# One-table layer norms, the last values inside the score loop's start, and a transposed inverse turned by VectorE, in a six-layer perceiver kernel

## The chip, the cores and the metric

The kernel runs on one core of one Trainium2 chip. The time is device microseconds of one execution. The kernel before took 768.55 us, the median of three runs (767.87 to 768.75).

## The reference

The input x is 128 x 256, the context 12544 x 256, all float32. Six residual layers follow one another, each on a layer norm of x:

```python
x = x + _L0_xattn_ref(_layernorm(x), ctx, mask, ...)   # 4 heads of 64, over the context
x = x + _L0_attn_ref(_layernorm(x), ...)               # gated delta net, 12 heads, 64 x 128 states
x = x + _L0_ffn_ref(_layernorm(x), ...)                # 8 experts, the best one
x = x + _L1_xattn_ref(_layernorm(x), ctx, ...)         # 16 heads of 16, over the context
x = x + _L1_attn_ref(_layernorm(x), ...)               # linear attention with a decay scan, gated
x = x + _L1_ffn_ref(_layernorm(x), ...)                # 8 experts, the best two

def _layernorm(x, axis=-1, eps=1e-05):
    m = jnp.mean(x, axis=axis, keepdims=True)
    v = jnp.var(x, axis=axis, keepdims=True)
    return (x - m) / jnp.sqrt(v + eps)
```

The delta net's step over 128 rows is a recurrence. The kernel solves it for all rows at once, which needs, for each head, the inverse of a 128 x 128 unit triangular matrix.

## The kernel before

The rows of x lie on the 128 partitions. The context is worked through in 24 blocks of 512 rows and one of 256. The first attention (`xattn0_first`) makes keys (L404), values (L417), scores (L438) and weighted sums (L465) block by block and keeps the context in SBUF. The second attention needs keys and values of the same context. They depend only on weights, so a `Filler` hands them out in small units as work for TensorE wherever it would wait: `fill(n)` issues the next n units. A block has eight of them: four for two key tiles `pk` (L1027, two units a tile), which ScalarE copies to `kh` (L1034) and a DMA stores in DRAM, and four for two value tiles `pv` (L1048), which ScalarE copies into the place of the context (L1053, shown as `ctx<-pv`). Both kinds rotate through two PSUM banks, so a third tile waits until ScalarE has copied the first.

From the first attention's end to the second attention's start the order on TensorE and ScalarE is the order of the code (`manual_schedule`); other engines are ordered by a scheduler. Whatever stands between two operations in the code stands between them in the queues.

**Layer norm** (`layernorm`, L134). VectorE computes mean and variance; ScalarE computes the inverse root as exp(-0.5 ln(v + eps)) (`rsqrt`); VectorE makes the normed `h`; TensorE transposes it (L151). Ln and Exp come from two function tables here, "natural_log" and "exp_and_others", each brought in by an ACT_TABLE_LOAD. Fill units are issued between these steps. The last two layers have a norm of their own (`root`, L1339 to L1351) with a Newton step behind the two activations and one table, "natural_log_exp_and_others", which holds both functions and is loaded once at the end of the second attention (L1137).

**The inverse** (L815 to L845). The 32 x 32 blocks on the diagonal are inverted by doubling, in four levels after a first one. `t` holds the inverse, `tt` its transpose, both in the tile `inv`. Each level multiplies in three sets of 48 small products, 96 passes on TensorE each:

```python
each(px, lambda r, h, c: am[r, h, :], t, four_tiles)
xs = block("xs")
nc.scalar.mul(xs, px, -1.0)
```

Then `py` from `tt` and `xs` is added to `t`, and `pyt` from `xs` and `tt` is added to `tt`, with two fill units behind each set. Afterwards blocks of 64 rows are put together in the same way (L874 to L891), from copies `t64` and `ttf` that POOL makes of `t` and `tt`. After level 0 `t` is made from `tt` by one VectorE transposition in blocks of 32 (L830).

**From the filler to the scores of the second attention.** `xattn1_first` computes queries and their maxima, issues all remaining units (`fill(None)`), gives the filler's two banks back (`close`), and calls `weigh1`. There each chunk of 128 context rows has 64 score products (L1101) into four banks, `st1` (one bank, one buffer) and `st3` (three banks, two buffers), two exponentials on ScalarE (L1107) into `e`, and the weighted sums (L1118) into the bank `ot`, which a product of zeros (L1091) clears first. Scores run two chunks ahead of the sums: scores(0), scores(1), then for each chunk i scores(i + 2) and the sums of i.

**The tail** (`last_layers`). After the last sums ScalarE copies `ot` (L1141). The result is turned and divided. `beat(n)` (L1359) issues n products of 256 columns, two passes each, whose result is never read. Seven of them stand ahead of the fifth layer's norm.

Of the kernel before, what the change touches and what calls it, by code (L numbers as in the profile page):

```python
# [11 lines left out]
F32 = mybir.dt.float32  # L12
# [3 lines left out]
AF = mybir.ActivationFunctionType  # L16
ALU = mybir.AluOpType
# [55 lines left out]
def network(ctx: ExitStack, tc: tile.TileContext, a: dict, y_out, bad):  # L73
# [45 lines left out]
        )  # L119


    def rsqrt(dst, src, bias, scale=1.0, fill=None):


        if fill:
            nc.scalar.preload_act_table_set("natural_log")
            fill(2)
        nc.scalar.activation(dst, src, AF.Ln, bias=bias, scale=scale)
        if fill:
            nc.scalar.preload_act_table_set("exp_and_others")  # L130
            fill(2)
        nc.scalar.activation(dst, dst, AF.Exp, scale=-0.5)

    def layernorm(x, psum, tag, fill=None):  # L134

        stats = small.tile([S, 6], F32, tag="ln_stats", name="ln_stats")
        nc.vector.bn_stats(stats, x)
        mv = small.tile([S, 2], F32, tag="ln_mv", name="ln_mv")
        nc.vector.bn_aggr(mv, stats)
        rstd = small.tile([S, 1], F32, tag="ln_rstd", name="ln_rstd")  # L140
        if fill:
            fill(1)
        rsqrt(rstd, mv[:, 1:2], eps[:S, 0:1], fill=fill)
        h = act.tile([S, D], F32, tag="h", name="h", bufs=1)
        nc.vector.tensor_scalar(h, x, mv[:, 0:1], rstd, ALU.subtract, ALU.mult)
        hT = act.tile([128, KC, S], F32, tag="hT", name="hT", bufs=1)
        if fill:
            fill(4)
        pt = psum.tile([128, 512], F32, tag=tag, name="ln_pt")
        for k in range(KC):  # L150
            nc.tensor.transpose(pt[:, k * S : (k + 1) * S], h[:, k * 128 : (k + 1) * 128], ident)  # L151
        nc.vector.tensor_copy(hT.rearrange("p k s -> p (k s)"), pt[:, : KC * S])
        if fill:
            fill(1)
        return hT
# [418 lines left out]
    def delta_net(x, wqkv, fill):  # L574
# [7 lines left out]
        with (  # L582
# [136 lines left out]
            nc.scalar.preload_act_table_set("exp_and_others")  # L719
# [105 lines left out]
            for li in range(len(LEVELS)):  # L825
                am = block("am")
                nc.gpsimd.tensor_mul(am, atc, m_blk[:, li, :].unsqueeze(1).to_broadcast([128, NH, 32]))
                if li == 0:
                    nc.vector.tensor_sub(tt, m_blk[:, len(LEVELS), :].unsqueeze(1).to_broadcast([128, NH, 32]), am)
                    nc.vector.transpose(  # L830
                        flat[:, :384], flat[:, 384:768]
                    )
# [12 lines left out]
                nc.vector.tensor_add(tt, tt, pyt)  # L845
                fill(2)


# [87 lines left out]
    def experts(x, wr, bias_row, we, be_src, top, y=None, fill=lambda n: None):  # L936

        with (
# [6 lines left out]

            be = mp.tile([NE, D], F32, name="be")
            nc.sync.dma_start(be, be_src)
            hT = layernorm(x, psp, "ps", fill)
# [115 lines left out]
    def weigh1(x, qs, kss, cp, sp, loaded, late):  # L1064

        H, DH, G = 16, 16, 4
        with (
            tc.tile_pool(name="x1_e", bufs=1) as ep,  # L1070
            tc.tile_pool(name="x1_st", bufs=1, space=PSUM) as ps_st,
        ):
            xb = cp.tile([S, D], F32, name="xb")
# [17 lines left out]
            nc.tensor.matmul(ot.rearrange("p g s -> p (g s)"), zl, zr, start=True, stop=False)  # L1091

            def scores(i):
                b, c = chunks[i]
                e = ws[i % 3]
                st1 = ps_st.tile([128, 1, G, S], F32, tag="st1", name="st1")
                st3 = ps_st.tile([128, 3, G, S], F32, tag="st3", name="st3", bufs=2)
                for g in range(G):
                    for j in (1, 2, 3, 0):
                        r = slice(32 * j, 32 * j + 32)  # L1100
                        nc.tensor.matmul(  # L1101
                            st3[:, j - 1, g, :] if j else st1[:, 0, g, :],
                            kss[b % 3][r, g // 2, g % 2, c * 128 : (c + 1) * 128], qs[r, g, :],
                            start=True, stop=True,
                        )
                for st, j in ((st1, slice(0, 1)), (st3, slice(1, 4))):
                    nc.scalar.activation(  # L1107
                        e[:, j].rearrange("p j g s -> p (j g s)"),
                        st.rearrange("p j g s -> p (j g s)"), AF.Exp,
                    )  # L1110
                return e
# [13 lines left out]
            for b in range(loaded, 2):  # L1125
                load1(kss, b)
            with tc.manual_schedule(engines={PE, ACT}):
                es = [scores(0), scores(1)]
                for i, (b, c) in enumerate(chunks):
                    if c == 0 and b + 2 < NB:  # L1130
                        load1(kss, b + 2)
                    if c == 0 and b == 12:
                        late()
                    if i + 2 < len(chunks):
                        es.append(scores(i + 2))
                    attend(i, es.pop(0))
                nc.scalar.preload_act_table_set("natural_log_exp_and_others")  # L1137

            oT = cp.tile([128, G, S], F32, name="oTs")
            for g in (0, 2):  # L1140
                nc.scalar.copy(oT[:, g : g + 2], ot[:, g : g + 2])  # L1141
            pt = ps_st.tile([128, 1, G, S], F32, tag="st1", name="pt")[:, 0].rearrange("p g s -> p (g s)")
# [55 lines left out]
    def xattn1_first(x, wq, filler, close, late):  # L1198

        fill = filler.fill  # L1200
        H, G = 16, 4
        with (
            tc.tile_pool(name="x1_c", bufs=1) as cp,
            tc.tile_pool(name="x1_s", bufs=2) as sp,
            tc.manual_schedule(engines={PE, ACT}),
        ):
            qs = cp.tile([128, G, S], F32, name="qs")
            kss = strips1(cp)
            load1(kss, 0)
# [98 lines left out]
    def last_layers(x, w, total):  # L1308
# [4 lines left out]
        with (  # L1313
# [114 lines left out]
            for m in range(KC):  # L1428
# [9 lines left out]
            nc.scalar.preload_act_table_set("natural_log_exp_and_others")  # L1438
            beat(2)
            away = both()  # L1440
            nc.vector.tensor_sub(away, o, v)
# [127 lines left out]
    class Filler:  # L1569
# [2 lines left out]

        def __init__(self, kp):
            self.kp, self.units = kp, self.steps()

        def steps(self):
            for b in range(NB if bad is not None else EARLY):
# [11 lines left out]
        def fill(self, n):  # L1589

            for _ in self.units if n is None else islice(self.units, n):
                pass

    with tc.tile_pool(name="k1", bufs=3) as kp:
        filler = Filler(kp)
# [136 lines left out]
```

## Time and profile before

| what | value |
|---|---|
| median of three runs | 768.55 us |
| profiled execution | 771.03 us |
| its span | 769.0 us |
| mean granted TensorE clock | 0.994 |
| DMA traffic, mean over the span | 74 GB/s |

| stage, us from the span's start | length | TensorE busy |
|---|---|---|
| first attention's loop, 30 to 265 | 235.00 | 234.49 |
| its end and the delta net's norm, 265 to 299 | 34.00 | 32.61 |
| delta net up to the inverse, 299 to 348 | 49.00 | 48.38 |
| inverse, 348 to 393 | 45.00 | 42.59 |
| rest of the delta net and the experts, 393 to 457 | 64.00 | 64.00 |
| second attention's norm and queries, 457 to 470 | 13.00 | 12.05 |
| remaining units, 470 to 523.3 | 53.30 | 53.30 |
| passage to the scores, 523.3 to 533.1 | 9.80 | 8.28 |
| score loop, 533.1 to 730 | 196.90 | 196.90 |
| end of the loop and the last two layers, 730 to 769 | 39.00 | 29.18 |

A matrix product of float32 runs as several passes, and the profile counts passes: one of 256 columns takes about 0.215 us, one of 512 about 0.43. In the profile's rows the bracket at the end gives how long the engine was idle before the row and what ended that time; "issue" means that nothing the profile shows was waited for. PE is TensorE's products, PEld its weight loads, DVE VectorE, ACT ScalarE, POOL GpSimd, SP the engine that issues most DMAs.

### The profile page before, as it was taken

To read this page: it belongs to the slowest core of one execution; us is meant where nothing else is said; L and a number is where in the kernel's file an instruction comes from. 1 tells how busy PE (TensorE), PEld (TensorE's weight loads), DVE (VectorE), ACT (ScalarE), POOL (GpSimd) and SP (SyncE) were. 2 spreads that over 40 slices of the span, in tenths; PEclk is the share of its full clock that TensorE was granted. 3 is DMA by queue.
4 is the path that set the end of the run, shared out by engine and by line. 5 is a ranking of instruction groups with operands and counts; after the bars stand their busy time and mean duration, and the time that the engine had idled before them with its cause. 6 is when DMAs were issued, how large, how long until landed. Compare 5 with 4: busy or idle time off the path is not lost.

```text
span 769.0 us, 23891 instructions
## 1 busy us (share of the span) xinstructions
PE 748.8 (97%) x10861; PEld 562.1 (73%) x10861; DVE 221.1 (29%) x405; ACT 406.9 (53%) x491; POOL 234.7 (31%) x192
## 2 busy tenths in 40 slices
PE   8999999999999999999999999999999999999985
PEld 4677777777777867666667757667888888888873
DVE  2444444433444444972114142000000000000045
ACT  2433433333444424654224432336999999999941
POOL 5686666667776632314012021000000000000000
PEclk9999999999999999999999999999999999999998
DMA  9970000000000012333010345211432222222000
GB/s 314 384 272 8 6 9 8 8 8 8 9 5 3 1 42 86 110 111 112 31 58 34 103 154 122 94 69 54 132 109 67 70 58 69 72 62 71 6 2 12
DMA packets 36126, 56.70 MB, mean 74 GB/s; under 512 B 5904, under 2 KB 12608, under 8 KB 36016
## 3 DMA queue, kind: packets, MB, share of 16 engines
q1 hardware_dynamic: 35648, 54.05, 22.0%
q8 instruction: 87, 1.43, 0.8%
q0 software_dynamic: 368, 1.03, 0.4%
q14 instruction: 23, 0.19, 0.1%
HBM read 42.09 MB, written 12.98 MB: 72 GB/s over the span
## 4 chain that ended last, share of the span: by engine, by line
PE 91%; DMA 3%; POOL 2%; ACT 2%; issue 1%; DVE 1%; SPq 0%; ACTq 0%; POOLq 0%; DVEq 0%
PE st L1101 14%; PE ot L1118 12%; PE pv L1048 11%; PE pk L1027 11%; PE pv L417 10%; PE pk L404 9%; PE st L438 6%; PE ot L465 6%; PE pr L634 1%; POOL e L451 1%; DMA msk<-in_maskT 1%; PE py L956 1%; PE spare L1359 1%; DMA row<-in_row 1%; DMA m<-in_mask 1%
## 5 line engine op out<-in xcount | busy, mean ns | idle before, releaser
L1107 ACT ACTIVATE e<-st 128x512 f32<-128x512 f32 x196 | 189.7, 1021 | 17.4 <-PE st L1101 16.1
L451 POOL TENSOR_TENSOR e<-e,mk 128x1024 f32<-128x1024 f32 x49 | 115.5, 2357 | 76.1 <-ACT e L445 62.8
L1101 PE MATMUL st<-qs,ks 32*128 32x128 f32 x3136 | 115.8, 283 | 0.8 <-ACT e L1107 0.8
L1101 PEld LDWEIGHTS st<-qs,ks 32*128 32x128 f32 x3136 | 96.9, 186 | 21.4 <-ACT e L1107 20.7
L1118 PE MATMUL ot<-e,ctx 128*17 128x128 f32 x3136 | 105.0, 274 | 0.0
L1048 PE MATMUL pv<-wv,ctx 128*128 128x256 f32 x392 | 92.8, 382 | 2.2 <-ACT kh L1034 1.6
L1027 PE MATMUL pk<-ctx,wk 128*128 128x512 f32 (+1 forms) x200 | 93.4, 591 | 0.8 <-ACT ctx L1053 0.8
L1048 PEld LDWEIGHTS pv<-wv,ctx 128*128 128x128 f32 x392 | 72.9, 190 | 23.5 <-issue 10.7
L456 DVE TENSOR_TENSOR sums<-sums,e 128x1024 f32<-128x1024 f32 x49 | 60.0, 1225 | 100.9 <-POOL e L451 100.9
L417 PE MATMUL pv<-wkv,ctx 128*128 128x256 f32 x392 | 88.3, 383 | 0.0
L1118 PEld LDWEIGHTS ot<-e,ctx 128*17 128x17 f32 x3136 | 77.6, 97 | 12.1 <-ACT e L1107 0.3
L404 PE MATMUL pk<-ctx,wkv 128*128 128x512 f32 (+1 forms) x200 | 86.4, 584 | 0.0
L445 ACT ACTIVATE e<-e 128x1024 f32<-128x1024 f32 x49 | 51.8, 1057 | 65.2 <-DVE e L444 62.4
L417 PEld LDWEIGHTS pv<-wkv,ctx 128*128 128x128 f32 x392 | 73.3, 190 | 11.7 <-PE sc L499 0.8
L447 POOL TENSOR_SCALAR mk<-msk 128x256 f32<-128x256 uint8 x49 | 68.3, 1395 | 4.1
L444 DVE TENSOR_TENSOR e<-st,nm 128x1024 f32<-128x1024 f32 x49 | 56.7, 1218 | 40.7 <-PE st L438 40.7
L1034 ACT ACTIVATE kh<-pk,col 128x512 f32<-128x512 f32 (+1 forms) x50 | 33.8, 679 | 64.7 <-PE pk L1027 63.7
L404 PEld LDWEIGHTS pk<-ctx,wkv 128*128 128x128 f32 x200 | 38.0, 190 | 40.7 <-issue 39.7
L1147 DVE RECIPROCAL den<-pt 128x16 f32<-128x16 f32 x1 | 0.3, 258 | 209.0 <-PE pt L1144 209.0
L1053 ACT COPY ctx<-pv 128x512 f32<-128x512 f32 x49 | 28.7, 586 | 53.8 <-PE pv L1048 53.7
L1027 PEld LDWEIGHTS pk<-ctx,wk 128*128 128x128 f32 x200 | 36.0, 190 | 28.4 <-issue 24.0
L408 ACT COPY kT<-pk 128x1024 f32<-128x1024 f32 (+1 forms) x25 | 24.9, 996 | 58.7 <-PE pk L404 58.7
(324 smaller groups left out, 622.9 us busy)
## 6 DMA issues: line engine op xcount, KB each, us to landing
ctx<-in_ctxT SPq DMA_DIRECT2D x24, 512.0 KB, 8.3
kd<-kh SPq DMA_DIRECT2D x48, 256.0 KB, 2.0
ks<-kd SPq DMA_DIRECT2D x192, 64.0 KB, 2.7
w<-in_L_ffn_expert_w SPq DMA_DIRECT2D x4, 512.0 KB, 3.8
ctx<-in_L_ffn_We SPq DMA_DIRECT2D x4, 512.0 KB, 4.0
msk<-in_maskT SPq DMA_DIRECT2D x24, 64.0 KB, 1.8
w<-in_L_attn_Wqk SPq DMA_DIRECT2D x2, 768.0 KB, 10.1
w<-in_L_attn_Wv SPq DMA_DIRECT2D x2, 768.0 KB, 10.1
```

Source lines behind the costliest of these rows:

```text
L404: nc.tensor.matmul(pk[:, m, :n], wkv[:, k, m * 128 : (m + 1) * 128], ctx_blocks[b][:, k, :], start=(k == 0), stop=(k == KC - 1),)
L417: nc.tensor.matmul(pv[:, i, c * D : (c + 1) * D], ctx_blocks[b][:, k, rows], wkv[:, k, D:], start=(k == 0), stop=(k == KC - 1),)
L444: nc.vector.tensor_add(e, st, nm.unsqueeze(2).to_broadcast([128, 4, 2, S]))
L445: nc.scalar.activation(e, e, AF.Exp)
L447: nc.gpsimd.tensor_scalar(mk, msk[:, c0 * 128 : (c0 + 2) * 128].rearrange("p (c s) -> p c s", c=2), 1.0, 0.0, ALU.mult, ALU.add,)
L451: nc.gpsimd.tensor_mul(e, e, mk.unsqueeze(1).to_broadcast([128, 4, 2, S]))
L456: nc.vector.tensor_add(sums, sums, e)
L1027: nc.tensor.matmul(pk, wk1[:, k, m * 128 : (m + 1) * 128], ctx_blocks[b][:, k, :], start=(k == 0), stop=(k == KC - 1),)
L1048: nc.tensor.matmul(pv[:, c, :], ctx_blocks[b][:, k, rows], wv1[:, k, :], start=(k == 0), stop=(k == KC - 1),)
L1101: nc.tensor.matmul(st3[:, j - 1, g, :] if j else st1[:, 0, g, :], kss[b % 3][r, g // 2, g % 2, c * 128 : (c + 1) * 128], qs[r, g, :], star ...
L1107: nc.scalar.activation(e[:, j].rearrange("p j g s -> p (j g s)"), st.rearrange("p j g s -> p (j g s)"), AF.Exp,)
L1118: nc.tensor.matmul(ot[32 * j : 32 * j + DH + 1, g, :], v[:, c, 8 * (g // 2) + 2 * j + g % 2, :], e[:, j, g, :], start=False, stop=(i + 1 = ...
```

## The change

- A function `log_and_exp` asks for the table that holds both Ln and Exp; the norms use it instead of two tables, and nothing is loaded where it is already in place. `layernorm` gains a Newton step of its own (`ln_ve`, `ln_t`) and issues its fill units as three before the two activations and two behind them (before: one, two and two). The other places that asked for "exp_and_others" (in `rsqrt` and at the key norms) or for the joint table (in the tail) call the function. The load at the end of the second attention goes.
- In the four levels of the inverse the `pyt` products, their addition and two fill units go; `tt` is made from `t` by the VectorE transposition.
- `xattn1_first` leaves the last two units, the last block's values. `weigh1` has its score banks in two pools as fixed tiles: `st_a`, `st1` and `ot` in one, `st_b` in the other, on the banks that the filler used. The order is scores(0), the last values (into the bank `ot`), scores(1), scores(2), clearing `ot`, the sums of 0; from there on as before.
- The beats ahead of the fifth layer's norm are five instead of seven.

```diff
+    def log_and_exp():
+        nc.scalar.preload_act_table_set("natural_log_exp_and_others")
...
-            nc.scalar.preload_act_table_set("exp_and_others")
+            log_and_exp()
...
-    def layernorm(x, psum, tag, fill=None):
+    def layernorm(x, psum, tag, fill=None, load=True):
...
+        nc.vector.tensor_scalar_add(ve, mv[:, 1:2], 1e-5)
+        if load:
+            log_and_exp()
         if fill:
-            fill(1)
-        rsqrt(rstd, mv[:, 1:2], eps[:S, 0:1], fill=fill)
+            fill(3)
+        nc.scalar.activation(rstd, mv[:, 1:2], AF.Ln, bias=eps[:S, 0:1])
+        nc.scalar.activation(rstd, rstd, AF.Exp, scale=-0.5)
+        nc.vector.scalar_tensor_tensor(t, rstd, rstd, ve, ALU.mult, ALU.mult)
+        nc.vector.tensor_scalar(t, t, -0.5, 1.5, ALU.mult, ALU.add)
+        nc.vector.tensor_mul(rstd, rstd, t)
+        if fill:
+            fill(2)
...
-                py, pyt = bank32("py"), bank32("pyt")
+                py = bank32("py")
                 each(py, lambda r, h, c: tt[r, h, :], xs, four_tiles)
                 nc.vector.tensor_add(t, t, py)
-                fill(2)
-                each(pyt, lambda r, h, c: xs[r, h, :], tt, four_tiles)
-                nc.vector.tensor_add(tt, tt, pyt)
+                nc.vector.transpose(flat[:, 384:768], flat[:, :384])
                 fill(2)
...
+            st_b = ps_sb.tile([128, 3, G, S], F32, name="st_b")
             ot = ps_st.tile([128, G, S], F32, name="ot")
-            nc.tensor.matmul(ot.rearrange("p g s -> p (g s)"), zl, zr, start=True, stop=False)
+            st1 = ps_st.tile([128, 1, G, S], F32, name="st1")
+            st_a = ps_st.tile([128, 3, G, S], F32, name="st_a")
...
-                es = [scores(0), scores(1)]
+                es = [scores(0)]
+                if rest:
+                    rest(ot)
+                es.append(scores(1))
...
                     if i + 2 < len(chunks):
                         es.append(scores(i + 2))
+                    if i == 0:
+                        nc.tensor.matmul(ot.rearrange("p g s -> p (g s)"), zl, zr, start=True, stop=False)
                     attend(i, es.pop(0))
-                nc.scalar.preload_act_table_set("natural_log_exp_and_others")
...
-                fill(None)
+                fill(filler.left - 2)
             close()
-            return weigh1(x, qs, kss, cp, sp, 2, late)
+            return weigh1(x, qs, kss, cp, sp, 2, late, filler.last)
...
-            beat(7)
+            beat(5)
...
+        def last(self, bank):
+            self.tile = lambda shape, name: bank.rearrange("p (c g) s -> p c (g s)", c=2)
+            self.fill(None)
```

More of the change, by code (lines that the diff above doesn't have):

```diff
@@ L140, in layernorm @@
         rstd = small.tile([S, 1], F32, tag="ln_rstd", name="ln_rstd")
+        ve = small.tile([S, 1], F32, tag="ln_ve", name="ln_ve")
+        nc.vector.tensor_scalar_add(ve, mv[:, 1:2], 1e-5)
+        if load:
+            log_and_exp()
         if fill:
-            fill(1)
-        rsqrt(rstd, mv[:, 1:2], eps[:S, 0:1], fill=fill)
+            fill(3)
+        nc.scalar.activation(rstd, mv[:, 1:2], AF.Ln, bias=eps[:S, 0:1])
+        nc.scalar.activation(rstd, rstd, AF.Exp, scale=-0.5)
+        t = small.tile([S, 1], F32, tag="ln_t", name="ln_t")
+        nc.vector.scalar_tensor_tensor(t, rstd, rstd, ve, ALU.mult, ALU.mult)
[3 more added lines that the diff above has]
+            fill(2)
         h = act.tile([S, D], F32, tag="h", name="h", bufs=1)
@@ L718, in delta_net @@
                 nc.scalar.activation(rn, pn, AF.Ln, bias=eps[:, 1:2])
-            nc.scalar.preload_act_table_set("exp_and_others")
+            log_and_exp()
             fill(2)
@@ L947, in experts @@
             nc.sync.dma_start(be, be_src)
-            hT = layernorm(x, psp, "ps", fill)
+            hT = layernorm(x, psp, "ps", fill, load=False)
             pl = psp.tile([128, 512], F32, tag="ps", name="pl")
@@ L1062, in load1, with weigh1 @@
                 nc.sync.dma_start(kss[b % 3][32 * j : 32 * j + 16, :, p, :n], src[j, p])
-    def weigh1(x, qs, kss, cp, sp, loaded, late):
+    def weigh1(x, qs, kss, cp, sp, loaded, late, rest=None):
         H, DH, G = 16, 16, 4
@@ L1070, in weigh1 @@
             tc.tile_pool(name="x1_e", bufs=1) as ep,
+            tc.tile_pool(name="x1_sb", bufs=1, space=PSUM) as ps_sb,
             tc.tile_pool(name="x1_st", bufs=1, space=PSUM) as ps_st,
@@ L1087, in weigh1 @@
             ws = [ep.tile([128, 4, G, S], F32, name=f"e{n}") for n in range(3)]
+            st_b = ps_sb.tile([128, 3, G, S], F32, name="st_b")
             ot = ps_st.tile([128, G, S], F32, name="ot")
-            nc.tensor.matmul(ot.rearrange("p g s -> p (g s)"), zl, zr, start=True, stop=False)
+            st1 = ps_st.tile([128, 1, G, S], F32, name="st1")
+            st_a = ps_st.tile([128, 3, G, S], F32, name="st_a")
             def scores(i):
                 b, c = chunks[i]
-                e = ws[i % 3]
-                st1 = ps_st.tile([128, 1, G, S], F32, tag="st1", name="st1")
-                st3 = ps_st.tile([128, 3, G, S], F32, tag="st3", name="st3", bufs=2)
+                e, st3 = ws[i % 3], (st_a, st_b)[i % 2]
                 for g in range(G):
@@ L1141, in weigh1 @@
                 nc.scalar.copy(oT[:, g : g + 2], ot[:, g : g + 2])
-            pt = ps_st.tile([128, 1, G, S], F32, tag="st1", name="pt")[:, 0].rearrange("p g s -> p (g s)")
+            pt = st1[:, 0].rearrange("p g s -> p (g s)")
             for g in range(G):
@@ L1437, in last_layers @@
                 )
-            nc.scalar.preload_act_table_set("natural_log_exp_and_others")
+            log_and_exp()
             beat(2)
@@ L1574, in __init__ @@
             self.kp, self.units = kp, self.steps()
+            self.left = sum(2 * KC + n // 128 for _, n in BLOCKS)
         def steps(self):
@@ L1591, in fill @@
             for _ in self.units if n is None else islice(self.units, n):
-                pass
+                self.left -= 1
+        def last(self, bank):
+            self.tile = lambda shape, name: bank.rearrange("p (c g) s -> p c (g s)", c=2)
+            self.fill(None)
     with tc.tile_pool(name="k1", bufs=3) as kp:
```

## The prediction

> **What bounds the kernel now.** I read the page's engine line and its chain first, then busy time by stretches, then the timeline wherever TensorE is not full.
>
> ```profile
> PE 748.8 (97%) x10861; PEld 562.1 (73%) x10861; DVE 221.1 (29%) x405; ACT 406.9 (53%) x491; POOL 234.7 (31%) x192
> ...
> PE 91%; DMA 3%; POOL 2%; ACT 2%; issue 1%; DVE 1%; SPq 0%; ACTq 0%; POOLq 0%; DVEq 0%
> ```
>
> TensorE (PE) is busy 97% of the span and carries 91% of the chain. Its queue is in order, so only two things shorten the run: less work on PE, or less waiting of PE. By stretches PE is full nearly everywhere: 234.49 of 235.00 us from 30 to 265, 53.30 of 53.30 from 470 to 523.3, 196.90 of 196.90 from 533.1 to 730. It idles at 288 to 299 (1.39), 348 to 393 (2.41), 457 to 470 (0.95), 523.3 to 533.1 (1.52) and in the tail. The change works in just these places. The timeline of two layer norms, ScalarE (ACT) above PE:
>
> ```profile
> 292.93 1.28 ACT L130 ACT_TABLE_LOAD   x1
> 294.22 0.59 ACT L1053 COPY ctx<-pv 128x512 f32<-128x512 f32 x1
> 294.86 1.98 PE L1027 MATMUL pk<-ctx,wk 128*128 128x512 f32 x4 [0.78 <-ACT ctx L1053]
> 458.50 1.28 ACT L130 ACT_TABLE_LOAD   x1
> 459.80 0.69 ACT L1034 ACTIVATE kh<-pk,col 128x512 f32<-128x512 f32 x1
> 460.54 1.99 PE L1048 MATMUL pv<-wv,ctx 128*128 128x256 f32 x8 [0.95 <-ACT kh L1034]
> ```
>
> A table load delays a copy out of PSUM, and PE waits for that bank: 0.78 and 0.95 us. The inverse, the passage into the scores, and the tail:
>
> ```profile
> 350.14 0.58 DVE L830 STREAM_TRANSPOSE inv<-inv 128x384 f32<-128x384 f32 x1
> 362.35 1.02 PE L815 MATMUL pyt<-inv,xs 32*32 32x32 f32 x96
> 363.30 1.99 PE L1048 MATMUL pv<-wv,ctx 128*128 128x256 f32 x8
> 371.92 0.47 PE L815 MATMUL pyt<-inv,xs 32*32 32x32 f32 x33 [0.22 <-issue]
> ```
> ```profile
> 523.28 1.89 PE L1048 MATMUL pv<-wv,ctx 128*128 128x256 f32 x8
> 525.89 0.37 PE L1091 MATMUL ot<-zr,zl 1*128 1x512 bf16 x1 [0.72 <-issue]
> 527.24 5.62 ACT L1107 ACTIVATE e<-st 128x512 f32<-128x512 f32 x6 [1.35 <-issue]
> 527.89 1.15 PE L1101 MATMUL st<-qs,ks 32*128 32x128 f32 x26 [0.61 <-ACT e L1107]
> 530.82 1.07 PE L1118 MATMUL ot<-e,ctx 128*17 128x128 f32 x32
> 539.42 1.94 ACT L1107 ACTIVATE e<-st 128x512 f32<-128x512 f32 x2 [0.16 <-PE st L1101]
> ```
> ```profile
> 733.05 1.28 ACT L1137 ACT_TABLE_LOAD   x1
> 734.34 0.65 ACT L1141 COPY oTs<-ot 128x256 f32<-128x256 f32 x2
> 736.62 4.97 PE L1359 MATMUL spare<-w,ident 128*128 128x256 f32 x14 [1.13 <-ACT total L1157]
> 738.55 0.35 DVE L1367 TENSOR_SCALAR ctx<-ident,ctx 128x128 f32<-128x128 f32 x1
> 736.60:740.00 3.40, 3.38 (x8) 2.76 (x9) 1.91 (x8) 0.50 (x2) 0.00 (x0) 0.50 0.01 2
> ```
>
> One set of pyt products takes PE from 362.35 to 363.30. In the passage PE stands still after the last values until ScalarE gives banks back. In the tail the spare products run until about 741.4, though their successor's operand is ready at 738.90; the last line, of the busy time by stretches (length, then busy PE, weight loads, VectorE, ScalarE, POOL, then the granted clock), shows a clock of 0.50 for 3.4 us there.
>
> **Part by part.** *The transposed inverse.* Four pyt sets go, 0.95 us each without a gap: 3.8 us. The twelve px, py and pyt sets hold five "issue" gaps of 0.43, 0.22, 0.68, 0.60 and 0.47 (2.40 us). Between them lie 383, 127, 383 and 128 passes, always a multiple of about 128, so I take them as tied to places in PE's instruction stream. Counted on in the changed order from the unmoved first gap, the next places fall 4.7, 2.9, 2.9 and 2.9 us apart (1.72 of fill units and some 1.2 of products each). Before, four of the six places 3.1 to 3.5 us after the one ahead had a gap. So I expect four gaps still, and only 0.4 us less: 4.2 us in all. Bounds: 2.8, if the closer places lengthen the gaps by 1.0; 5.2, if gaps fall by 1.4.
>
> What replaces it: per level VectorE (DVE) does the add (0.56) and a transposition (0.58) instead of two adds of 0.56. The next px needs only the add, ready some 0.7 us after py (0.12 lag and 0.56); two fill units of 0.86 lie between, so it costs nothing. Without that cover it would cost 0.7 a level. The transposed half is ready 1.3 us after py and first read over 4 us later; behind it on DVE stands only the next add, on POOL the ttf copies, read 10 us later. POOL's last mask product sits behind a memset that waits for a block's last fill unit, yet comes some 5 us before its px. The eight fill units that stood around the products (0.86 each) move into the stretch from 470, which is full of the same work: they lengthen it as much as they shorten this. Their key stores move behind the expert weights on SP's queue; they are read tens of us later.
>
> *Layer norms.* Eight of seventeen table loads go (one of them in the tail, below). At the delta net's entry the copy held until 294.22 can start right behind PE at about 292.3, before the bank is wanted at 294.08: 0.78 us. At the second cross attention likewise 0.95. The Newton step adds three one-column operations on DVE, about 0.75 us by the tail's 0.22, 0.15 and 0.16 with their lags, ahead of h; the two missing loads more than repay that, and PE takes the transposes of h only when its fill units are done: at the experts PE is full from 433 to 457, h moves from 438.85 to about 437.4, and nothing is gained or lost. The first norm is likewise under the keys (h 8.06, transposes 10.07): nothing. In the fourth norm POOL's memsets run until 461.67 and h took 1.20 instead of 0.41; if the small operations stall until then, h is ready at about 462.3, just when PE wants it. Bounds for the two gains together: 0.6 and 2.2; I take 1.73.
>
> The Trainium skill's "ScalarE: Activation LUTs", What ACT_TABLE_LOAD costs, puts a switch at 1283 ns plus a drain of about 1380 ns. Here the row after the load at 292.93 starts 0.01 us after its end, so I see no such drain; by the page eight loads would be about 21 us of ScalarE time, by the rows 10.3. Since PE's waits are what counts, the sum is the same by both.
>
> *Last values between the scores.* Call the old start of the last values T (523.28). Now scores(0) runs at T, into banks long free; ScalarE begins its exponentials at T+1.35 instead of T+3.96. The values run from T+1.1 to T+2.8, scores(1) to T+3.9; scores(2) waits for the single st1 bank until T+4.75 (the values' copy, 0.59, stands before the second exponentials on ScalarE) and ends at T+5.65; clearing ot 0.3; the first ot products at T+5.95 against T+7.54. Gain 1.5, bounds 0.7 (copy and exponentials clash more) and 2.2 (all idling goes). The loop behind it has the same order and banks.
>
> *Tail.* The load at 733.05 ends as the last ot products end (734.14) plus the usual 0.2 us lag: gain 0, at most 0.2. Five beats instead of seven drop four passes that ran at full clock, 0.215 each: 0.86, to about 740.5, still behind the operand at 738.90. Bounds: 0, if the lower clock then reaches into the projections; 2.4, if no low clock falls here.
>
> The Trainium skill's "TensorE: Matmul & The Clock Gate", Part 1, says that the clock rises after one busy window of 3.4 us and that these windows run freely. The 3.4 us row at 0.50 fits. It speaks against fewer beats: five beats at half rate are an estimated 4.3 us, little above one window, and the window's phase differs from run to run.
>
> **The sum.** 4.2 + 1.73 + 1.5 + 0 + 0.86 = 8.3 us. The profiled execution took 771.03 (span 769.0 and 2.0 around it), so it would take 762.7. The median of the runs is 2.48 below the profiled one; I keep that distance: 768.55 - 8.3 = 760.2. All small ends together give 4.1 less (764.5), all large ones 12.2 less (756.4).
>
> **Rivals.** *A, the clock is kind:* no low clock in the beats. Half rate cost 8 passes 0.215 each, of which 1.5 is to be had before 738.90 binds: 758.7. For it: only 1.9 of 3.4 us were idle before the drop; against: it did drop. *B, half the gain:* the inverse saves only its lower 2.8, POOL's memsets hold the fourth norm, the passage gives 0.7, the beats 0.4: 763.9. *C, slower:* the 196 exponentials of the second attention run under the joint table instead of "exp_and_others". ScalarE has 0.16 us of slack in each 2.10 us of 98 chunks. If that table's exponential is more than 8% slower, ScalarE becomes the bound; above 13% (another 0.085 x 98 = 8.3) the whole gain is gone; at 25% it is 98 x 0.33 = 32 us more: 792. Against: Ln under another table took 0.69 for 128x512 and so did a biased copy, so tables seem not to set the rate. *D, it does not happen:* excluded by the changed kernel's instruction order, which has nine loads and no pyt sets in the levels.
>
> **Chances.** Forecast 0.75, A 0.10, B 0.10, C 0.03, and 0.02 for some new wait that takes all back. A measurement of this kernel tells about 0.2% (1.5 us) from no change. Forecast and A lie wholly below 767.0 and B nearly: faster 0.92, same 0.03, slower 0.05 (C and the new wait). The range holds forecast, A and B without their far ends: 757.2 to 764.0.
>
> **What would show it.** Right: no wait above 0.2 us on PE at the two norms; between the first px and the 64-row products some 11 us less; transpositions of 0.58 on DVE with PE never waiting for DVE there; exponentials starting about 2.6 us earlier after the last pk; ScalarE still 1.94 a chunk; spare products ending 0.9 earlier. Wrong: chunks longer than 2.10, "issue" gaps in the inverse above 3.4 us, PE waiting for h, or half clock behind the beats.

## The result, and the profile after

The changed kernel takes 759.96 us (median of four runs, 759.24 to 760.74) against 768.65 for the kernel before (four runs, 767.87 to 771.19: the three of the table above and one more): a ratio of 0.9882, 95% interval 0.9856 to 0.9907. The forecast was 760.2, the range 757.2 to 764.0. The profiled execution took 759.24, its span 757.4.

In some executions of any of these kernels TensorE's clock falls to half for some 3.4 us in the beats, and the time is 1 to 2 us longer. Of the fourteen profiled executions the four with a mean granted clock of 0.994 or 0.995 show it, before among them (0.994), and the ten with 0.996 to 0.998 do not, after among them (0.998). So the two spans differ by 11.6 us where the medians differ by 8.7. "With the clock kept" below means the median of the executions at 0.997 or more: 768.73 for before (10 of the 19 in one series), 759.62 for after. All fourteen also show a clock of 0.50 in their last 2 to 6 us; from the fifth norm's product to the end it is 27.5 to 27.9 us in all of them, so this costs nothing that can be seen.

The page of after, the engines and the chain:

```profile
PE 740.8 (98%) x10473; PEld 556.5 (73%) x10473; DVE 224.9 (30%) x421; ACT 397.0 (52%) x483; POOL 234.4 (31%) x192
...
PE 95%; POOL 2%; DVE 1%; ACT 1%; issue 1%; POOLq 0%; DVEq 0%; ACTq 0%
```

388 passes are gone from PE, and its share of the chain rises from 91 to 95%: the change took away waits and work on PE. The places, each by the timeline. First the two norms on PE, before and then after:

```profile
288.67 3.69 PE L1048 MATMUL pv<-wv,ctx 128*128 128x256 f32 x16 [0.61 <-DVE x_xattn L570]
297.54 0.38 PE L151 MATMUL ln_pt<-ident,h 128*128 128x128 f32 x2
450.95 0.69 PE L1007 MATMUL pb<-be,wT 8*128 8x256 f32 x2
463.23 0.38 PE L151 MATMUL ln_pt<-ident,h 128*128 128x128 f32 x2
```
```profile
288.95 3.69 PE L1062 MATMUL pv<-wv,ctx 128*128 128x256 f32 x16 [0.60 <-DVE x_xattn L586]
292.48 3.60 PE L1041 MATMUL pk<-ctx,wk 128*128 128x512 f32 x8
296.77 0.38 PE L167 MATMUL ln_pt<-ident,h 128*128 128x128 f32 x2
437.23 0.69 PE L1021 MATMUL pb<-be,wT 8*128 8x256 f32 x2
443.98 3.62 PE L1062 MATMUL pv<-wv,ctx 128*128 128x256 f32 x16
448.29 0.38 PE L167 MATMUL ln_pt<-ident,h 128*128 128x128 f32 x2
```

The brackets of 0.78 and 0.95 are gone (0.60 or 0.61 stands in both kernels). Now read the starts, not the brackets. From the values' start to `ln_pt` it is 296.77 - 288.95 = 7.82 us; before it was 297.54 - 288.67 = 8.87: 1.05 less for a bracket of 0.78. At the second cross attention, from `pb` (the experts' bias, the last product ahead of this norm's stretch) to `ln_pt`, it was 463.23 - 450.95 = 12.28 and is 448.29 - 437.23 = 11.06: 1.22 less for 0.95. The inverse: the first px of the levels and the first px of the step behind them (from 32 rows to 64) in before, then PE and VectorE after:

```profile
355.99 1.02 PE L815 MATMUL px<-inv,am 32*32 32x32 f32 x96
393.77 0.95 PE L815 MATMUL px<-inv,at 32*32 32x32 f32 x48
```
```profile
355.24 1.02 PE L831 MATMUL px<-inv,am 32*32 32x32 f32 x96
358.10 1.30 PE L831 MATMUL py<-xs,inv 32*32 32x32 f32 x96
359.47 0.56 DVE L858 TENSOR_TENSOR inv<-inv,py 128x384 f32<-128x384 f32 x1 [9.52 <-PE py L831]
360.06 0.58 DVE L859 STREAM_TRANSPOSE inv<-inv 128x384 f32<-128x384 f32 x1
375.06 0.27 PE L831 MATMUL px<-inv,am 32*32 32x32 f32 x9 [1.25 <-issue]
380.05 0.95 PE L831 MATMUL px<-inv,at 32*32 32x32 f32 x48
```

Add and transposition lie under the units, and PE never waits for VectorE. One "issue" gap of 1.25 is left as a row; two more hide in sets that took longer than 0.95 (358.10 to 359.33, and 369.86 to 370.96, each to the start of the next row). From the first px of the levels to the first px of the 32-to-64 step ("the levels" from here on) it is 24.81 us instead of 37.78, of which 6.9 are the eight fill units that moved. The passage, ScalarE and PE; T, the start of what follows the last keys, is 515.32 here:

```profile
516.56 0.60 ACT L1123 ACTIVATE e<-st 128x512 f32<-128x512 f32 x1 [0.52 <-PE st L1117]
520.24 0.37 PE L1117 MATMUL st<-qs,ks 32*128 32x128 f32 x1 [0.50 <-ACT e L1123]
521.54 1.07 PE L1134 MATMUL ot<-e,ctx 128*17 128x128 f32 x32
```

Exponentials at T + 1.24, first sums at T + 6.22 (before: 7.54). Between them the scores of chunk 2 wait 0.50 for st1. The loop behind is as full as it was (from 522 to 720 PE is busy all 198.00 us, with 6040 passes), and a chunk still takes 2.10 us, so the joint table's exponential is no slower. The tail:

```profile
724.61 0.65 ACT L1162 COPY oTs<-ot 128x256 f32<-128x256 f32 x2 [1.17 <-PE ot L1134]
726.95 2.42 PE L1380 MATMUL spare<-w,ident 128*128 128x256 f32 x10 [1.20 <-ACT total L1178]
729.65 0.71 PE L1392 MATMUL ln_pt<-ctx 128*128 128x128 f32 x4 [0.28 <-DVE ctx L1388]
```

Without the load the copy starts 0.05 us behind the last sums (724.56) instead of 0.20. Five beats at full clock end before VectorE's operand: PE now waits 0.28 for it. VectorE itself stands idle for 0.47 us between the norm's two statistics operations there, 0.10 in before, and the profile names nothing that it waited for.

Summed over the stages the two profiled executions differ by 13.0 in the levels (6.9 of it are the eight units that moved, so 6.1), 2.3 at the norms, 1.2 in the passage, 2.0 in the tail: 11.6. The forecast had 4.2, 1.73, 1.5 and 0.86. What is luck of these two executions and what is the change, the runs tell.

### The profile page after: what moved, and what is told of

It reads as the page before. It is cut to its first block, busy times and chain, and to the rows that moved or that the text cites. A ratio compares the mean times of both kernels' runs of the same rounds, so it can differ in the third digit from the quotient of the medians.

```text
span 757.4 us, 23122 instructions
## 1 busy us (share of the span) xinstructions
PE 740.8 (98%) x10473; PEld 556.5 (73%) x10473; DVE 224.9 (30%) x421; ACT 397.0 (52%) x483; POOL 234.4 (31%) x192
## 4 chain that ended last, share of the span: by engine, by line
PE 95%; POOL 2%; DVE 1%; ACT 1%; issue 1%; POOLq 0%; DVEq 0%; ACTq 0%
PE ot L1134 13%; PE pk L1041 11%; PE pv L1062 11%; PE pv L433 11%; PE pk L420 10%; PE st_b L1117 7%; PE st_a L1117 7%; PE st L454 6%; PE ot L481 6%; PE pr L650 1%; POOL e L467 1%; PE py L970 1%; PE st L1117 1%; PE pg L780 1%; PE py L1494 1%; PE pout L944 1%
## 5 line engine op out<-in xcount | busy, mean ns | idle before, releaser
L1117 PE MATMUL st<-qs,ks 32*128 32x128 f32 x784 | 113.0, 283 | 0.5 <-ACT e L1123 0.5
L1117 PEld LDWEIGHTS st<-qs,ks 32*128 32x128 f32 x784 | 94.4, 186 | 0.7 <-ACT e L1123 0.7
L1062 PE MATMUL pv<-wv,ctx 128*128 128x256 f32 x384 | 90.1, 382 | 1.2 <-ACT kh L1048 0.6
L1123 ACT ACTIVATE e<-st_a 128x1536 f32<-128x1536 f32 x49 | 70.8, 1445 | 0.0
L1123 ACT ACTIVATE e<-st_b 128x1536 f32<-128x1536 f32 x49 | 70.8, 1445 | 0.0
L1123 ACT ACTIVATE e<-st 128x512 f32<-128x512 f32 x98 | 58.5, 597 | 17.0 <-PE st L1117 17.0
L1117 PE MATMUL st_a<-qs,ks 32*128 32x128 f32 x1176 | 57.3, 283 | 0.0
```

The lines of the kernel that those rows point to most:

```text
L1062: nc.tensor.matmul(pv[:, c, :], ctx_blocks[b][:, k, rows], wv1[:, k, :], start=(k == 0), stop=(k == KC - 1),)
L1117: nc.tensor.matmul(st3[:, j - 1, g, :] if j else st1[:, 0, g, :], kss[b % 3][r, g // 2, g % 2, c * 128 : (c + 1) * 128], qs[r, g, :], star ...
L1123: nc.scalar.activation(e[:, j].rearrange("p j g s -> p (j g s)"), st.rearrange("p j g s -> p (j g s)"), AF.Exp,)
```

## The experiments

The theory that I took into them: the inverse is worth more than 4.2, because every interruption of the units' stream costs PE something by itself and because the issue gaps shrink; the tail's 2.0 is mostly the clock. The rival: the three parts are worth what was forecast and all the rest is the clock. The runs came in three series on three chips, each with its own runs of before (medians 769.14, 769.56 and 769.45), so a difference of under 1 us between kernels of different series is read from the traces.

**One part alone: the inverse.** The kernel before with this edit only:

```diff
-                py, pyt = bank32("py"), bank32("pyt")
+                py = bank32("py")
...
-                fill(2)
-                each(pyt, lambda r, h, c: xs[r, h, :], tt, four_tiles)
-                nc.vector.tensor_add(tt, tt, pyt)
+                nc.vector.transpose(flat[:, 384:768], flat[:, :384])
```

> The kernel before with the change in the inverse alone (no pyt sets, a VectorE transposition, eight fill units fewer there). By the prediction's step: 4.2 us less, 764.4, and from the first px of the levels to the px of the 64-row step's predecessor (37.78 us before) 37.78 - 4.2 - 6.9 (eight units of 0.86 that move to the stretch from 470) = 26.7. By the reading of the changed kernel's trace (24.81 there): 6.1 us less, 762.5: four sets of 0.95 (3.8), four interruptions of the units' stream fewer at 0.19 each (a pair of units takes 1.91 between small products and 1.72 in the dense stretch; 0.8), and 1.5 from shorter or fewer issue gaps. If the extra gain was only the clock in the tail of the profiled run, the inverse gives 4.2 and its stretch still takes 26.7.

Measured: 763.37 us, ratio 0.9924 (0.9907 to 0.9941); with the clock kept 763.20, 5.5 less than before. The levels took 26.03, the stretch up to the last keys grew by exactly the 6.88 of eight units. 26.03 lies between the two readings: the gaps came to 3.1 us here (26.03 less eight sets at 2.87), against 1.9 in the profile of after with the same order. So 6.1 was partly luck, but 4.2 is too little. This one order shows four gaps (0.19, 0.30, 0.26 and 1.52).

**One part alone: the norms.** The one-table `layernorm`, `log_and_exp` and the missing load behind the loop, put into the kernel before.

> The kernel before with the one-table layer norms alone (Newton step, eight loads fewer, the load behind the score loop gone). By the prediction: 1.73 us less, 766.9, with the waits of 0.78 at the delta net's entry and 0.95 at the second cross attention gone and nothing else moved. By the reading of the changed kernel: 1.9 us less. A rival says that the load at the loop's end counts too: another 0.2 to 1.3 less, seen as ot's copy starting right behind the last sums.

Measured: 766.28, ratio 0.9961 (0.9947 to 0.9974); with the clock kept 766.12, 2.6 less. Both waits are gone, with 1.04 and 1.22 us between the same starts as above. From the first sums to ScalarE's copy of ot it is 203.06 us; in the kernels with the inverse or the passage alone, which keep the load at the loop's end, 203.21. Between the last sums and this copy lie 0.05 us without the load and 0.20 with it: the load counted 0.15. The stretch itself also varies (203.52 in before, with the load, and 203.23 in the kernel with three units below, without it).

**One part alone: the passage.** Two pools, fixed banks, the last values behind scores(0), in the kernel before (its table load behind the loop stays).

> The kernel before with the last values between the scores alone (two pools, fixed banks). By the prediction: 1.5 us less, first sums 5.95 us behind the end of the last keys (7.54 before). By the reading of the changed kernel: 1.3 less, sums at 6.22. Rival: the fixed banks change the score loop; then a chunk is no longer 2.10 us and the time moves by 98 times the difference.

Measured: 767.55, ratio 0.9977 (0.9968 to 0.9987); with the clock kept 767.54, 1.2 less. From the last keys' copy to the first sums 6.07 us instead of 7.29, and the loop no longer than before (203.21 us against 203.52). The three parts alone come to 5.5 + 2.6 + 1.2 = 9.3 us; all of the change with the clock kept, the beats included, gives 9.1.

**Seven beats again.** `beat(7)` in the changed kernel.

> The changed kernel with seven beats again instead of five. At full clock the spare products end 0.86 later; since the changed kernel's products already wait 0.28 for VectorE's operand behind five, the time is 0.5 us longer if the clock stays up, and up to 2.1 longer (the difference between the two profiled tails, 4.80 and 2.70 us from the first spare product to the norm's) if the clock falls in the beats as it did before. Rival, the beats keep the clock up: with five it falls behind them in some executions, so that seven are as fast or up to 1 us faster.

Measured: 759.86, ratio to before 0.9877 (0.986 to 0.9893): the same as with five. The timeline of this kernel's tail:

```profile
727.19 3.29 PE L1380 MATMUL spare<-w,ident 128*128 128x256 f32 x14 [1.20 <-ACT total L1178]
730.32 0.61 PE L1392 MATMUL ln_pt<-ctx 128*128 128x128 f32 x4
```

From the first spare product to the norm's product it is 3.13 us, as in all three one-part kernels (3.12, 3.12, 3.13); with five it is 2.70. The 4.80 of before was the half clock. So fewer beats are worth 0.43 here at full clock, too little for the times to show. Part of what they could give is lost to the 0.47 us in which VectorE stands idle: in the kernel without a Newton step below VectorE has no such gap (0.10), and the same five beats take 2.34.

**Three units instead of two** behind each set in the changed kernel's levels.

```diff
                 nc.scalar.mul(xs, px, -1.0)
-                fill(2)
+                fill(3)
...
                 nc.vector.transpose(flat[:, 384:768], flat[:, :384])
-                fill(2)
+                fill(3)
```

> The changed kernel with three fill units instead of two behind each set of small products in the four levels: eight units more there and eight fewer in the stretch from 470. If an interruption costs 0.19 us however long it is, the time stays (760.0) and the stretch from the first px to the 32-to-64 step is 24.8 + 6.9 = 31.7. If the cost is per unit (0.095), it is 32.5 and the time 0.8 longer. The issue gap, at pass 87 of the fourth px, 375.06 us: if it is tied to a place in PE's instructions, it comes some 18 passes earlier in the same px (six units of two or four passes stand ahead of it) and 5 us later; if it is tied to the time or to traffic, it stays near 375 us, in the work that is there then, or is gone.

Measured: 757.39, ratio 0.9839 (0.9823 to 0.9855), 2.6 us less than the changed kernel by the medians of two chips. The gap is gone, which a fixed place alone does not allow; traffic could. The timeline of PE:

```profile
377.08 1.02 PE L831 MATMUL px<-inv,am 32*32 32x32 f32 x96
380.81 1.02 PE L831 MATMUL py<-xs,inv 32*32 32x32 f32 x96
```

The busy time of its levels (length, busy PE with its passes, clock, then the DMA engines' share and GB/s):

```profile
354.69:384.55 29.86, 29.86 (x842) 1.00 0.16 57
```

Set to set 3.73 us: 0.95 for the set and 2.78 for three units, where two took 1.92. A unit is 0.86 and an interruption 0.2, however many units it has. Eight times 3.73 is the whole 29.86. The changed kernel without gaps would have 8 x 2.87 = 22.96; it had 24.81, and 25.10, 25.19 and 25.19 in the other kernels here with the same levels, the last two on this run's chip. So the third unit is worth 1.8 to 2.2 us by the traces.

**No cover.** All four units behind px, none behind py.

```diff
                 nc.scalar.mul(xs, px, -1.0)
-                fill(2)
+                fill(4)
...
                 nc.vector.transpose(flat[:, 384:768], flat[:, :384])
-                fill(2)
```

> The changed kernel with all four units behind px and none behind py, so that nothing covers VectorE's add. By the prediction's price (0.7 us a level where the next px waits for the add alone, 0.12 + 0.56): four waits, 2.8 us more; four interruptions fewer give 0.8 back: 2.0 longer, 762.0. Rival: the next px waits for the transposition too, 1.3 a level, 5.2 - 0.8 = 4.4 longer. Second rival: nothing, since TensorE has the waits elsewhere anyway.

Measured: 762.04, ratio 0.9911 (0.9889 to 0.9933), 2.1 more than the changed kernel; levels of 27.24 instead of 24.81 (25.19 in the two kernels on the same chip). The timeline:

```profile
361.62 1.01 PE L831 MATMUL px<-inv,am 32*32 32x32 f32 x96 [0.75 <-DVE inv L858]
```

PE waits for the add (L858), not for the transposition (L859): 0.75 three times and 0.65 once, 2.9 us. The forecast's price of a missing cover holds.

**No Newton step.** The four small operations on VectorE left out of `layernorm`.

> The changed kernel without the Newton step in the four layer norms (the last digits of the norm differ). The prediction had it hidden everywhere: same time (760.0), h about 0.75 us earlier in each norm. Rival: it stands in the way at the two norms where TensorE waited before, at the delta net's entry and at the second attention: 0.75 to 1.5 us less.

Measured: 759.29, ratio 0.9862 (0.9845 to 0.9878), within the scatter of the changed kernel. The traces decide: from the values' start to `ln_pt` at the delta net's entry 297.00 - 289.17 = 7.83 (7.82 with it), and from the 64-row step to the last keys 127.91 in both. At the first norm the transposes come behind the same eight key products in both, 2.4 and 3.2 us after h began. The step is hidden in all four norms.

**Clearing ot ahead of scores(2).**

```diff
+                    if i == 0:
+                        nc.tensor.matmul(ot.rearrange("p g s -> p (g s)"), zl, zr, start=True, stop=False)
                     if i + 2 < len(chunks):
                         es.append(scores(i + 2))
-                    if i == 0:
-                        nc.tensor.matmul(ot.rearrange("p g s -> p (g s)"), zl, zr, start=True, stop=False)
```

> The changed kernel with the clearing of ot ahead of scores(2) instead of behind it. TensorE waits 0.50 us there for ScalarE to free st1; the clearing (0.3) would lie in that wait: first sums 5.9 us behind the last keys instead of 6.22, time 0.3 less, which the time can't show but the trace can. Rival: the clearing waits for the copy of the last values and the wait only changes its name: 6.2.

Measured: 759.72, ratio 0.9869 (0.9853 to 0.9886). From the last keys' copy to the first sums 5.84 us instead of 6.06 (6.00 instead of 6.22 from T): 0.22, seen in the trace alone.

**Where the issue gaps come from.** With the gaps gone at three units I formed another theory: PE is sent instructions no faster than some 31 to 34 passes a us, and the small products want 35.6 with two units between them. Four kernels for it.

> The changed kernel with one unit instead of two behind each set: eight units fewer in the levels, still 0.86 + 0.19 behind py against the 0.7 of VectorE's add. Theory of supply: TensorE wants about 49 passes a us and gets some 34, so the levels (about 790 passes) take 23 us instead of the gap-free 16, with gaps of about 7 us in all where the changed kernel has 1.9: 5 us longer, about 765. If the gaps hang on places alone: four to six gaps of the same size, about 760. If a cover goes (ScalarE's negation behind px), it shows as PE waiting for xs, 0.1 to 0.3 a level.

One unit instead of two. Measured: 766.09 (764.2 in the two executions with the clock kept), ratio 0.9951 (0.9938 to 0.9965). What PE waited for in and around the levels (us in all, times, longest):

```profile
PE py L831 <- issue: 4.7, 4, 1.4
PE px L831 <- issue: 1.9, 2, 1.1
```

The busy time of the levels:

```profile
354.81:377.75 22.94, 17.09 (x793) 1.00 0.08 27
```

Forecast 23, measured 22.94; 16.05 without gaps. Six gaps stand some 128 passes apart (pass 90 of the first py, 21 of the second, 48 of the third px, and so on), and work goes on after them at 358.98, 363.80, 367.35, 371.19, 375.78 and 379.23 (the last already in the step behind): 3.45 to 4.82 us from one to the next, 4.05 in the mean. PE never waits for xs. The DMA engines are busy 0.08 of the time here and 0.16 in the gap-free levels, so the gaps do not come from more traffic.

> The changed kernel with three units behind px and two behind py. Theory of supply: TensorE takes up to 30.4 passes a us for long without a gap (5988 in 196.9 us of the score loop) and 28.2 in the gap-free levels with three units; with two units it wants some 35.6 and, gaps counted, gets 33 to 35. Here it wants 31.4: at most one small gap, the stretch from the first px to the 32-to-64 step 26.4 to 26.8 us, time 757.5 to 758.0. Rival, the gaps hang on places of the stream (every 128 passes) and on what stands there: one gap of about 1 us stays in the fourth px, time 759.

Three units behind px and two behind py. Measured: 758.57 (758.14 with the clock kept), ratio 0.9858 (0.9833 to 0.9884). The levels took 26.99, more than the 26.4 to 26.8 expected, with one gap, in the fourth px at 375.74: a bracket of 0.41, and 0.6 by the length of its set. One gap is what the theory allowed, and its place is the rival's, at half of the rival's size; the time lies between the two. This run does not decide.

> The kernel before with three fill units instead of two behind each of the twelve sets in the levels. Theory of supply: no gaps, twelve times 3.73 = 44.8 us for the stretch (37.5 to 37.8 with gaps and twelve units fewer), 2.4 to 3.4 us less time: about 766.0. Then the pyt sets by themselves are worth what lies between this kernel and one that differs by the inverse alone, 4 x (0.95 + 0.19) = 4.6. Rival, places of the stream: gaps of 0.2 to 0.7 stay, 768.5.

Three units behind the twelve sets of the kernel before. Measured: 767.03, ratio 0.9964 (0.9952 to 0.9976); with the clock kept 766.14, 2.8 less than before on the same chip (768.98). Levels of 44.76 us, no gap. Against the 29.86 of the changed kernel with three units that is 14.90, of which 10.32 are twelve units: 4.58 us is what four pyt sets cost when no gap disturbs, 4 x (0.95 + 0.19).

> The changed kernel with both edits that gained: three fill units behind each set in the levels, and the clearing of ot ahead of scores(2). If the issue gaps come from a supply of instructions that the denser order outruns, and the two add up: no gap in the levels, first sums 5.85 us behind the last keys' copy, 757.2 us, 2.5 less than the changed kernel and some 11.7 less than the kernel before. Rival: the gap-free run before was a lucky one; then gaps come back in some executions and the median is about 759.

Both gains together in the changed kernel. Measured: 756.99 (756.4 to 757.27), ratio to before 0.9835 (0.9814 to 0.9856): 3 us better than the changed kernel by the medians of two chips (2.0 to 2.4 by the traces: 1.8 to 2.2 in the levels and 0.22 in the passage), and the best version here. Levels 29.84 and first sums at 5.84, as in the kernels with one of the edits each, so the gap-free order was not luck.

The traces that all these runs left show what the gaps wait for. Each page lists a DMA queue of instructions (packets, MB, share of the DMA engines), here the one of after:

```profile
q8 instruction: 84, 1.38, 0.8%
```

Before has 87 packets, each of 16,384 bytes. Divided among PE's passes and weight loads that is some 250 a packet in both kernels (21722 in 87, 20946 in 84), and the three packets fewer go with the 388 passes and their weight loads that are gone; so I take it as PE's queue. In the profiled executions 33 "issue" gaps stand in the levels and at the start of the step behind them, and after every one work goes on 1.20 to 1.60 us behind the end of such a packet, while the packets follow one another at 3.3 to 5.6 us there. In the kernel with one unit packets end at 357.61, 362.46, 366.15, 369.82, 374.43 and 377.76, and its six gaps end 1.37, 1.34, 1.20, 1.37, 1.35 and 1.47 us later. In the kernel with three units the same six places of the stream come 1.31 to 4.11 us behind their packets, and there is no gap. So a gap is PE waiting for its next block of instructions: it opens at a fixed place, every 128 passes, when that place is reached before the block is there.

## Why the prediction was right, point by point

**The sum.** Forecast 8.3 us, measured 8.7 by the medians and 9.1 with the clock kept. By the traces the terms are 5.2 (inverse) + 2.26 (norms) + 1.2 (passage) + 0.15 (tail load) + 0.43 (beats) = 9.2, the forecast ones off by 0.15 to 1.0, in both directions. That the sum came within 1 us is in part luck.

**Inverse, 4.2 forecast, 5.2 measured: mis-sized.** The pass time (four sets of 0.95) was right. Left out was that a set also interrupts the units' stream, 0.19 each time, 0.8 in all: fill pairs that I priced at 1.72 take 1.92 there. The gaps, by the lengths of the sets (the brackets that I summed, 2.40 for before, show less): over the kernels with the old levels 3.34, 3.06 and 2.34 us, over those with the new ones 1.85, 2.14, 2.23, 2.23 and 3.07. The means differ by 0.6, where 0.4 was forecast. 3.8, 0.8 and 0.6 are the 5.2; the inverse alone gave 5.5 by the times, and single pairs of traces give 3.9 to 6.1, since the gaps vary. That gaps stand at places about 128 passes apart was right, and that the distance in time to the place ahead decides; that four must come was not, one to four rows are seen. The Trainium skill's "Runtime: NRT & Kernel Launch", Instruction fetch mechanics, says that an engine's instructions are refilled in blocks of 256; with a weight load for each pass that is 128 passes, the spacing seen. It calls the cost of a new block mostly hidden; where the block is used up in less than some 4 us these runs show otherwise, 6.9 us in the kernel with one unit. This case's traces agree on the size (some 250 passes and weight loads a packet, gaps about 128 passes apart).

**Norms, 1.73 forecast, 2.26 measured: mis-sized.** The waits went, and nothing took their place: h came in time, also under POOL's memsets, where `h` itself stretched to 1.69 us while the one-column operations kept their 0.22, 0.15 and 0.16. But I took a bracket for the cost of a wait. It counts from the modelled end of the row ahead, and the next row could have started before that end (rows that follow without a wait start 0.1 to 0.2 us before the end of the one ahead); the start-to-start times say 1.04 and 1.22 for brackets of 0.78 and 0.95. The difference, 0.26 and 0.27, is near the interruption's 0.19; whether it is the same thing is not shown.

**Last values, 1.5 forecast, 1.2 measured.** The order came as worked out: exponentials 2.7 us earlier (2.6 said), scores(2) waiting for st1. The values took 1.92 instead of the 1.7 summed (the pair's price in the levels too), st1 came free at T + 4.92 instead of T + 4.75, the rest of scores(2) took 1.0 instead of 0.9, and the first sums stood at T + 6.22 instead of T + 5.95 (1.32 earlier by T, 1.23 by the last keys' copy).

**Tail load, 0 forecast, at most 0.2; 0.15 measured. Beats, 0.86 forecast, 0.43 measured.** The step that failed is the base: I priced the beats by the profiled execution, where the clock fell, but took the median's distance to it (2.48 us) as untouched. That distance probably held the kept clock already: the clocks of those three runs are not on record, but their 768.55 is near the 768.73 of the later runs with the clock kept. And at full clock five beats end before VectorE's operand, which its own idle 0.47 us delays; without it they would give 3.13 - 2.34 = 0.8, near the forecast. Rival A, a kind clock in the beats, was the case in three of the changed kernel's four runs, and not in one of ten; it moved the time little because most of its price was in that distance. Half clock cost 4.80 - 3.13 = 1.7 us with seven beats, 3.95 - 2.70 = 1.25 with five.

**B and C** fell: of B's parts only the beats gave half (0.43), and chunks stayed at 2.10 us. Errors of opposite sign in the terms (1.0 and 0.5 too little, 0.3 and 0.4 too much) kept the sum within 1 us.

**Open.** Why the packets come at 3.3 us here and at 5.6 us there, so that the gaps of one and the same order differ by 1.2 us between kernels that differ elsewhere; what VectorE's idle 0.47 us in the tail is; and which executions lose the clock: by the mean granted clock before lost it in 9 of 19 executions of one series, 14 of 20 of another and at least 5 of 7 of the third, the kernels with one part changed in 4 of 26. The place of the tail's idle time in windows of 3.4 us may decide it: in before, in the kernel with one unit and in before with three units the half clock of the beats lasted 3.413 us and full clock then 23.893, seven times as long. That was not tried.

## What to carry to other kernels

Price a wait or a change of shapes on TensorE by start to start of the rows around it, not by its bracket: here a break of the stream cost some 0.2 to 0.3 us more. A dense run of very small products can outrun its own instructions; where "issue" gaps stand at equal counts of passes, put a little more of other work between the sets (here a third unit: 2.6 us by the medians, 1.8 to 2.2 by the traces). And when a profiled execution differs from the median, look which part of it the clock explains before a term is priced from it.

## What the runs showed that I had not expected

- TensorE kept up 30.5 passes a us for 198 us in the score loop (6040 in 198.00) and 28.2 in the levels with three units, without a gap; it wanted 31.3 and had one gap of 0.41; it wanted 35.6 and had 1.9 to 3.3 us of gaps; it wanted 49 and got 34.6 (793 in 22.94).
- Gaps stood 128 passes apart, and in the densest order the next stretch began 3.45 to 4.82 us behind the one ahead.
- All 33 "issue" gaps in the levels and right behind them ended 1.20 to 1.60 us after a 16,384-byte packet of the instruction queue.
- A gap can hide inside a row: a set of 96 passes shown as 1.30 us without a bracket, where others show 1.02, and 1.23 us to the next row's start, where others take 0.95.
- In the fourteen profiled executions a mean granted clock of 0.994 or 0.995 went with half clock in the beats, 0.996 and more with full clock there.
